# A weights' Walsh transform on one engine, and the pacing of two stages where they meet: a four-layer Mamba and sedenion network on one core

## The chip, the cores and the metric

The kernel runs on one core of a Trainium2 chip. The metric is device time in microseconds of one execution, taken as a median over runs; the median before is 10949.66 us (three runs, 10944.49 to 10950.38). The profile is of one execution with a span of 10943.5 us.

## The reference

The input x is 4 x 192 x 64 x 64, fp32. Four layers are applied to it in turn. Cut to what matters:

```python
# layer 0: tokens of 192 channels, 4096 per image, LayerNorm, then two Mambas
xs = layernorm(x.reshape(b, -1, c))
x = (xs + mamba(xs, m1) + mamba(flip(xs, -1), m2)).reshape(b, c, w, h)
# one Mamba: xz = x @ in_w.T; short causal convolution; silu; B, C, dt from x_w, dt_w; then
#   h = exp(dt * A) * h + dt * x * B ;  y = sum_n h * C       (a scan over 4096 tokens, 16 states)
# layer 1: one Mamba over tokens, then per image
x1 = x + mamba(layernorm(x))
x2 = x1 + gelu(bn(depthwise3x3(x1)))
x = x2 + mlp(layernorm(x2))            # 192 -> 768 -> 192
# layer 2: masked 3x3 depthwise convolution (4 taps), its weights made from the image's own mean
wt = (relu(bn(x.mean((2, 3)) @ w1.T)) @ w2.T + b2) * MASK
x = conv(x, wt) + bias
# layer 3: windows of 4x4, a sedenion product of the 16 window positions with 16 weights
xw = window(layernorm(x)) @ sedenion_full_weight(w_sed)
x = x + gelu(unwindow(xw)) @ proj_w + proj_b
x = x + mlp(layernorm(x))
```

The 16 x 16 sedenion product is computed as a Walsh-Hadamard convolution plus a correction for the terms whose sign differs from it. For that, the 16 weight matrices of 192 x 192 are Walsh-transformed once, each with a sign of its own; the signs of the weights are `W_SIGNS = "------------+-+-"`.

## The kernel before, in words

The program has three stages. `two_mambas` is layer 0, `mamba_block` is layer 1, and `conv_and_windows` is layers 2 and 3. Instructions are issued in an order that Python generators write out by hand; each engine (TensorE, VectorE, ScalarE, GpSimd, and the SyncE queue that issues nearly all transfers) then runs its own instructions strictly in that order, and waits for others through semaphores. So what stands behind what on one engine is decided when the program is built.

**First stage.** Units of 512 tokens go through two Mambas in turn. `Scans` issues one 128 x 512 scan at a time; work of the next units (normalisation `norm`, projections `front`, output `back`) sits in lanes of a `Behind` object and is issued between the scans. Ahead of the first scan stand the first unit's normalisation, then `at_first(work)`, which is `walsh_weights`, then the first unit's `front`.

`front` multiplies by in_w on TensorE (L456), copies the result from PSUM on ScalarE (L459), clears the halo of the convolution on GpSimd (L451) and copies it in front (L452), convolves by matmuls with diagonal weights (L474), applies silu (L486), makes dt (L500 to L509), multiplies (L510, GpSimd), and stores the rows dt and dt*x to DRAM from the SyncE queue (L515, tiles r_dt and r_dtx). `load` (L535) reads them back, spread over states, as dtE and dtxE; the first VectorE operation on them is the product L565, and the scans L578 follow.

`walsh_weights` works on four blocks: two values of i (the main 128 channels and the remaining 64, held twice) times two column halves of n = 96. For each block it loads 128 x 16 x 96 weights (L904, tile w_raw), flips the signs of the two positive ones on ScalarE (L907), then runs four butterfly stages, bits 8, 2, 1 and 4, each of one addition and one subtraction (L918), between two tiles w_walsh, and stores the result to DRAM (L922). All loads and stores are on the SyncE queue, in program order, so a block's load is issued after the store of the block before it. The blocks with i = 0 run on VectorE, those with i = 1 on GpSimd: `engine = nc.gpsimd if i else nc.vector`.

**Second stage.** Units of 512 tokens again, one Mamba. After the scan of a unit come `back` (the output projection, into a strip of image rows) and `tail`: nine depthwise matmuls for each channel half (L1044, tile ps_dw), batch norm and gelu on ScalarE (L1053, L1063), the addition on GpSimd (L1067), LayerNorm through matmuls (`NormT.run`, L294 to L341), and then `end`, the MLP (`MlpT.run`: ps_h L363, evacuation to hid L368, gelu L375, ps_o L382). Its last operation, L1079, adds the residual and accumulates the channel sums that layer 2 needs; then the tile is stored (L1090).

Between scans, `Behind.tick` issues work: it counts rounds, gives each round a TensorE budget (2.1 us here), honours the wait that a piece asks for (`Piece.wait`), and issues a deferred evacuation (`later`) when its round has come. When the scans are over, two tails and what belongs to them remain. `Behind.drain` issues these: in each round it issues everything deferred at once, forces one piece of the first lane that can go, and calls `beside` with that piece's TensorE estimate.

**Third stage.** `conv_and_windows` is a generator. When the scans are over, `mamba_block` calls `next(following)` once, which sets up its lanes, loads the first half of the first image (L1178 and L1180, tile img), makes the layer 2 weights of images 0 to 2 (`weights`), and adds `prepare(0)` to a lane. From then on these lanes share the program with the second stage's drain. `prepare(b)` handles eight groups g of two window positions: for each of three channel chunks one tap on ScalarE (helper line L1280, tile xw) and three on VectorE (L1327), then a store (L1330, kept). `first_norm` follows: mean by matmuls (helper line L1272), subtraction (L1287, L1289), square (L1290), variance by matmuls, square root (L1295), reciprocal (L1296), scaling on GpSimd (L1297, L1299), gain and sign on ScalarE (L1280, tile xn), then `both` (L1367 to L1370) and the butterfly additions `settle` (L1381, L1382). The tile img has one buffer, so the second half of an image is loaded when groups 0 to 3 have read the first.

When `drain` is through, the generator goes on: the transformed weights w_main and w_side (L1573, L1575), the untransformed ones sed (L1578) and a pack of the projections t_bw (L1161) are loaded on the SyncE queue; all eight groups of the first image are run to their end; `weights` is made for image 3 (L1203 to L1223, with the sums of the last tails); sed gets its signs on ScalarE (L1587); and `spectrum` (L1420, tile sed_ps) begins. After it come `product`, `project` and `mlp` for each group, with the next image's `prepare` in a lane beside.

The functions that the change touches, before:

Of the kernel before, what the change touches and what calls it, by code (L numbers as in the profile page):

```python
# [15 lines left out]
AF = mybir.ActivationFunctionType  # L16
ALU = mybir.AluOpType
# [105 lines left out]
def near_convolution():  # L123


    sign = sedenion_signs()
    a, b = ([1 if v == "+" else -1 for v in text] for text in (X_SIGNS, W_SIGNS))
    s, rest = [], []
    for k in range(16):
        row = [sign[i][k] * a[i] * b[i ^ k] for i in range(16)]  # L130
        s.append(1 if sum(row) >= 0 else -1)
        rest.append([i for i in range(16) if row[i] != s[k]])
    return a, b, s, rest


class Lanes:
# [24 lines left out]
    def drain(self):  # L161
        self.until(lambda: not any(self.lanes))
# [12 lines left out]
class Behind:  # L175
# [83 lines left out]
            if not any(self.try_lane(n, True, True) for n in range(len(self.lanes))):  # L259
                assert until() or self.pending, "stuck"  # L260

    def drain(self, beside=None):

        while any(self.lanes) or self.pending:
            self.now += 1
            self.issue(True)
            p = next(filter(None, (self.try_lane(n, True, True) for n in range(len(self.lanes)))), None)
            assert p or self.pending or not any(self.lanes), "stuck"
            if p and beside:
                beside(p.pe)  # L270


class NormT:
# [614 lines left out]
def walsh_weights(nc, work, w_ap, out):  # L888


    _, w_sign, _, _ = near_convolution()
    n = C // 2

    def flat(t):
        return t.rearrange("p a b -> p (a b)")[:, : 16 * n]

    def split(v, bit):
        return v.rearrange("p (h e l) -> p e h l", e=2, l=bit * n)

    for i in range(2):  # L900
        for at in range(0, C, n):
            raw = work.tile([128, 4, T], F32, name="w_raw", tag="h", bufs=3)
            v = flat(raw).rearrange("p (j c) -> p j c", c=n)
            nc.sync.dma_start(v, w_ap[:, i, :, at : at + n])  # L904
            for j in range(16):
                if w_sign[j] > 0:
                    nc.scalar.activation(v[:, j, :], v[:, j, :], AF.Copy, scale=-1.0)  # L907
            t = [flat(work.tile([128, 4, T], F32, name="w_walsh", tag="h_apart", bufs=2)) for _ in range(2)]
            src = flat(raw)
            engine = nc.gpsimd if i else nc.vector  # L910
            for m, bit in enumerate((8, 2, 1, 4)):
                a, dst = split(src, bit), t[m % 2]
                for e, op in enumerate((ALU.add, ALU.subtract)):
                    p, o = slice(0, 128), split(dst, bit)[:, e]
                    if i and bit == 4:
                        p = slice(64 * e, 64 * e + 64)
                        o = dst[p, : NP * n].rearrange("p (h l) -> p h l", h=2)
                    engine.tensor_tensor(o, a[p, 0], a[p, 1], op)  # L918
                src = dst
            rows = slice(16, 16 + NP) if i else slice(0, 16)  # L920
            k = NP if i else 16
            nc.sync.dma_start(out[:, rows, at : at + n], src[:, : k * n].rearrange("p (j c) -> p j c", c=n))  # L922


def mamba_block(tc, x, p96, p96_ap, p128, p128_ap, m_in, ex_aps, out, sums, following):
# [3 lines left out]
    nc = tc.nc  # L929
    with ExitStack() as ctx:  # L930
# [195 lines left out]
        behind.add(1, norm(units[1]))  # L1126
        Scans(nc, stream, behind).run()
        scans.close()
        lanes, passed = next(following), [0.0]

        def beside(pe):
            passed[0] += pe
            while passed[0] > 1.0:
                passed[0] -= 1.0
                lanes.tick()

        behind.drain(beside)


# [467 lines left out]
def program(ctx, tc, aps, packs, out):  # L1607
# [6 lines left out]
    def m_ins(name):  # L1614
# [8 lines left out]
        (aps["spread"], aps["gather"]),  # L1623
        x1.rearrange("b (t c) -> b t c", c=C),
        lambda work: walsh_weights(tc.nc, work, aps["sed"], walsh),
    )
    with tc.manual_schedule():
        last = conv_and_windows(tc, x2, sums, packs, aps, walsh, out)
        mamba_block(
            tc,  # L1630
            x1.rearrange("b (c t) -> b c t", t=L),
            packs["a96"],
            aps["a96"],
            packs["a128"],
            aps["a128"],
            m_ins("m"),
            (aps["spread"], aps["gather"]),
            x2,
            sums,
            last,  # L1640
        )
        for _ in last:
            pass
# [118 lines left out]
```

## Time and profile before

| what | value |
|---|---|
| median of 3 runs | 10949.66 us |
| PE, DVE, ACT, POOL busy | 84%, 83%, 60%, 65% of the span |
| 0 to 140 us: PE, DVE, ACT, POOL busy | 41.0, 24.0, 22.0, 34.9 us |
| 140 to 5410 us (first stage's scans) | DVE 5097.7 of 5270 us, granted clock 0.77 |
| 5410 to 9030 us (second stage) | PE 3261.6, DVE 2991.2 of 3620 us, clock 0.88 |
| 9030 to 9285 us (the seam to the third stage) | PE 148.1, DVE 135.1, ACT 86.8 of 255 us, clock 0.74 |
| 9285 to 10943 us (third stage) | PE 1445.4 of 1658 us, clock 0.94 |

The table's last five rows come from the profile's busy time by stretches. PE is TensorE's matmuls, DVE is VectorE, ACT is ScalarE, POOL is GpSimd, SPq is the SyncE queue. The granted clock is the share of full speed that the throttle gave TensorE. A timeline line gives start and length in us, the engine, the line of the kernel, the operation, the tile written and those read, a count where several were merged, and in brackets the idle time of the engine ahead of it with what ended it.

### The profile page before, as it was taken

How to read it: one execution, taken by the hardware profiler on the slowest of the kernel's cores; microseconds unless marked ns; L12 is line 12 of the kernel's file. 1: busy time of each engine (PE TensorE's matmuls, PEld its weight loads, DVE VectorE, ACT ScalarE, POOL GpSimd, SP SyncE). 2: the span in 40 equal slices, each digit the busy share in tenths (PEclk: the TensorE clock that was granted, in tenths of full speed). 3: DMA queues.
4: the chain of work that ended last, by engine and by line, in shares of the span. 5: the costliest groups of instructions: out<-in, count | busy, mean ns of one | idle time of the engine just before them, and what ended most of it. 6: DMA issues, size and time to landing. Idle time of an engine off the chain costs nothing. (4 is left out here: it accounts for less than half of the span.)

```text
span 10943.5 us, 97569 instructions
## 1 busy us (share of the span) xinstructions
PE 9194.5 (84%) x31352; PEld 3651.3 (33%) x31352; DVE 9081.9 (83%) x7914; ACT 6568.9 (60%) x9794; POOL 7060.3 (65%) x2704
## 2 busy tenths in 40 slices
PE   5888888888888888888678999999999986889898
PEld 1222222222222322322223333333333332445555
DVE  5999999999999999999788888888878885555552
ACT  4666666666666666666466666656656653444443
POOL 5888888888888888888666656656656661111100
PEclk7777777777777777777678989889889887999999
DMA  4666666666666666666454545545444543122110
GB/s 127 182 177 175 182 178 173 183 179 173 182 179 175 182 177 175 182 178 174 127 160 133 140 127 140 134 126 140 129 134 132 138 110 78 37 57 64 41 41 18
DMA packets 969560, 1515.13 MB, mean 138 GB/s; under 512 B 244346, under 2 KB 277150, under 8 KB 968534
## 3 DMA queue, kind: packets, MB, share of 16 engines
q1 hardware_dynamic: 968190, 1505.85, 51.3%
q8 instruction: 247, 4.05, 0.2%
q10 hardware_dynamic: 856, 3.05, 0.1%
q14 instruction: 267, 2.19, 0.1%
HBM read 1295.45 MB, written 213.12 MB: 138 GB/s over the span
## 5 line engine op out<-in xcount | busy, mean ns | idle before, releaser
L578 DVE TENSOR_TENSOR_SCAN h<-dA,m_state,h 128x512 f32<-128x512 f32 x3840 | 4669.3, 1267 | 486.3 <-ACT dA L572 424.4
L594 POOL TENSOR_TENSOR h<-h,C 128x2048 f32<-128x2048 f32 x960 | 4347.2, 4533 | 601.6 <-ACT m_state L591 496.8
L572 ACT ACTIVATE dA<-dtE,m_A 128x512 f32<-128x512 f32 x4608 | 3106.0, 687 | 1322.0 <-DVE h L578 1204.4
L565 DVE TENSOR_TENSOR h<-dtxE,B 128x2048 f32<-128x2048 f32 x960 | 2171.9, 2262 | 150.1 <-DMA dtxE<-r_dtx 137.4
L603 PE MATMUL y<-h,gather 128*32 128x512 f32 x7680 | 1286.0, 748 | 414.1 <-POOL h L594 341.7
L456 PE MATMUL ps_in<-xT,m_in_w 96*128 96x512 f32 x1536 | 943.3, 762 | 294.6 <-ACT raw L459 176.9
L1297 POOL TENSOR_TENSOR d<-d,rs 128x512 f32<-128x512 f32 x64 | 86.0, 1344 | 1604.3 <-DVE rs L1296 1583.6
L474 PE MATMUL ps_conv<-raw,m_conv 128*128 128x512 f32 x2112 | 990.7, 618 | 12.6 <-POOL raw L452 10.9
L578 DVE TENSOR_TENSOR_SCAN h_apart<-dA,m_state,h_apart 128x512 f32<-128x512 f32 x768 | 922.8, 1261 | 42.5 <-ACT dA L572 42.5
L594 POOL TENSOR_TENSOR h_apart<-h_apart,C 128x2048 f32<-128x2048 f32 x192 | 870.3, 4533 | 43.7 <-ACT m_state L591 42.3
L565 POOL TENSOR_TENSOR h_apart<-dtxE,Bs 128x2048 f32<-128x2048 f32 x192 | 892.3, 4648 | 6.0 <-ACT Bs L554 6.0
L456 PEld LDWEIGHTS ps_in<-xT,m_in_w 96*128 96x128 f32 x1536 | 352.7, 242 | 862.5 <-issue 418.0
L474 PEld LDWEIGHTS ps_conv<-raw,m_conv 128*128 128x128 f32 x2112 | 419.1, 202 | 611.0 <-issue 564.4
L593 POOL COPY m_state<-h 128x4 f32<-128x4 f32 x384 | 71.8, 187 | 850.6 <-DVE h L578 814.6
L1044 PE MATMUL ps_dw<-strip,dw 96*96 96x512 f32 x1152 | 577.0, 648 | 1.3 <-ACT x L1053 0.9
L603 PEld LDWEIGHTS y<-h,gather 128*32 128x32 f32 x7680 | 165.0, 117 | 1221.0 <-POOL h L594 540.7
L510 POOL TENSOR_TENSOR raw<-dt,xc 128x1536 f32<-128x1536 f32 x96 | 330.1, 3438 | 296.3 <-ACT dt L509 296.3
L490 PE MATMUL ps_x<-xc,m_pack 128*44 128x512 f32 x576 | 351.3, 758 | 197.7 <-ACT xc L486 194.4
L1462 PE MATMUL sed_ps<-xn,sed 64*128 64x256 f32 (+3 forms) x2944 | 486.0, 403 | 7.0 <-DVE y L1481 7.0
L572 ACT ACT_TABLE_LOAD x345 | 442.6, 1283 | 6.2
L456 PE MATMUL ps_in<-xn,m_in_w 96*128 96x512 f32 x768 | 398.5, 665 | 47.8 <-ACT z L459 31.4
L382 PE MATMUL ps_o<-hid,t 128*96 128x512 f32 x768 | 391.3, 649 | 40.0 <-ACT hid L375 19.6
(196 smaller groups left out, 12239.7 us busy)
## 6 DMA issues: line engine op xcount, KB each, us to landing
dtE<-r_dt SPq DMA_DIRECT2D x2304, 256.0 KB, 5.0
dtxE<-r_dtx SPq DMA_DIRECT2D x2304, 256.0 KB, 4.1
r_dt<-dt SPq DMA_DIRECT2D x96, 768.0 KB, 4.0
r_dtx<-raw SPq DMA_DIRECT2D x96, 768.0 KB, 5.4
x<-x SPq DMA_DIRECT2D x64, 384.0 KB, 3.9
img<-x SPq DMA_DIRECT2D x28, 512.0 KB, 8.5
xt<-in_x SPq DMA_DIRECT2D x32, 384.0 KB, 5.5
x<-o SPq DMA_DIRECT2D x32, 384.0 KB, 4.9
```

The source lines that it names most:

```text
L382: nc.tensor.matmul(ps, self.w2[:, m, bass.ts(k, CP)], h[:, m, :], start=(m == 0), stop=(m == NH - 1),)
L456: nc.tensor.matmul(ps, self.in_w[:, k, bass.ts(e, 128)], xn[:, k, :], start=(k == 0), stop=(k == 1))
L474: nc.tensor.matmul(ps, self.conv[:, d, j, :], raw[:, d, j : j + T], start=(j == 0), stop=(j == K - 1))
L490: nc.tensor.matmul(ps, self.x_w[:, d, :], xc[:, d, :], start=(d == 0), stop=(d == ND - 1))
L510: nc.gpsimd.tensor_tensor(dtx, dt, xc, ALU.mult)
L565: engine.tensor_tensor(h, u["rows", k // 2, 1], u[B, k % 2].unsqueeze(1).broadcast_to([128, 4, T]), ALU.mult)
L572: self.nc.scalar.activation(dA, u["rows", k // 2, 0][:, j, :], AF.Exp, scale=self.A[:, k, j : j + 1])
L578: self.nc.vector.tensor_tensor_scan(h[:, j, :], u.pop(("dA", k, j)), h[:, j, :], self.state[:, k, j : j + 1], ALU.mult, ALU.add,)
L594: nc.gpsimd.tensor_tensor(h, h, u["C", k % 2].unsqueeze(1).broadcast_to([128, 4, T]), ALU.mult)
L603: self.nc.tensor.matmul(u["ys"][32 * j : 32 * j + 32, :], self.ex.gather[:, i // 2, :], h[:, j, :], start=(i == 0), stop=(i == 3 and not s ...
L1044: nc.tensor.matmul(ps, dw[:, k, j, :], s[:, k, dy : dy + rows, dx : dx + HW], start=(j == 0), stop=(j == 8),)
L1462: nc.tensor.matmul(out, sed[p, int(h is not None), i ^ position(k, s), cols], xn[b, g][p, c, :], start=group(t) not in begun, stop=left[gr ...
```

## The change: all Walsh blocks on VectorE with the signs in the first stage, and a drain that uses the pace of the scans

The first part takes the transform off ScalarE and GpSimd. The sign flips disappear: where a weight of the upper half has the other sign, the addition and the subtraction of the bit 8 stage change places. That needs one pair of instructions for each run of equal signs. In the upper eight these runs are 4, 1, 1, 1, 1 long, so the stage becomes two instructions of 384 and eight of 96 elements. The four blocks all run on VectorE. It is meant to keep ScalarE and GpSimd free for the first unit's front.

The second part replaces the drain's own loop by `tick(True)`, the loop that is used between scans, with its waits, its budget and its due rounds, and gives the third stage's lanes two ticks in every round, whether or not a piece of the tails went. It is meant to mix the last tails and the third stage's first groups evenly.

```diff
-    def drain(self, beside=None):
+    def drain(self, beside=lambda: None):
         while any(self.lanes) or self.pending:
-            self.now += 1
-            self.issue(True)
-            p = next(filter(None, (self.try_lane(n, True, True) for n in range(len(self.lanes)))), None)
-            assert p or self.pending or not any(self.lanes), "stuck"
-            if p and beside:
-                beside(p.pe)
+            self.tick(True)
+            beside()
...
+    turns = [0] + [l for l in range(1, 8) if w_sign[8 + l] != w_sign[7 + l]] + [8]
+    turns = list(zip(turns, turns[1:]))
...
-            for j in range(16):
-                if w_sign[j] > 0:
-                    nc.scalar.activation(v[:, j, :], v[:, j, :], AF.Copy, scale=-1.0)
...
-            engine = nc.gpsimd if i else nc.vector
             for m, bit in enumerate((8, 2, 1, 4)):
                 a, dst = split(src, bit), t[m % 2]
+                if bit == 8:
+                    for first, last in turns:
+                        at_l, ops = slice(n * first, n * last), (ALU.add, ALU.subtract)
+                        for e, op in enumerate(ops[::-1] if w_sign[8 + first] > 0 else ops):
+                            nc.vector.tensor_tensor(
+                                split(dst, bit)[:, e, 0, at_l], a[:, 0, 0, at_l], a[:, 1, 0, at_l], op
+                            )
+                    src = dst
+                    continue
...
-                    engine.tensor_tensor(o, a[p, 0], a[p, 1], op)
+                    nc.vector.tensor_tensor(o, a[p, 0], a[p, 1], op)
...
-        lanes, passed = next(following), [0.0]
-
-        def beside(pe):
-            passed[0] += pe
-            while passed[0] > 1.0:
-                passed[0] -= 1.0
-                lanes.tick()
+        lanes = next(following)
+
+        def beside():
+            lanes.tick()
+            lanes.tick()
```

More of the change, by code (lines that the diff above doesn't have):

```diff
@@ L892, in walsh_weights @@
     n = C // 2
+    assert max(w_sign[:8]) < 0
+    turns = [0] + [l for l in range(1, 8) if w_sign[8 + l] != w_sign[7 + l]] + [8]
+    turns = list(zip(turns, turns[1:]))
     def flat(t):
```

## The prediction

> **What bounds the kernel now.** I read the page's 40 slices first: no engine bounds the whole span. Up to slice 19 DVE stands at 9, then PE and DVE share, and from slice 34 PE stands at 8 to 9. The two stretches that the change touches are the seams before and between these regimes, where the average shares say nothing, so I read the timeline there.
>
> First seam, 0 to 140 us. The timeline of all engines (start, length, engine, line and operation, then the idle time before it and its releaser):
>
> ```profile
> 25.49 5.96 PE L456 MATMUL ps_in<-xT,m_in_w 96*128 96x512 f32 x8
> 28.53 5.55 DVE L918 TENSOR_TENSOR w_walsh<-w_walsh 128x768 f32<-128x768 f32 x6
> 34.52 1.68 SPq L904 DMA_DIRECT2D w_raw<-in_sed  x1
> 42.05 0.46 ACT L907 ACTIVATE w_raw<-w_raw 128x96 f32<-128x96 f32 x2 [15.41 <-DMA w_raw<-in_sed]
> ...
> 62.06 10.92 POOL L918 TENSOR_TENSOR w_walsh<-w_walsh 128x768 f32<-128x768 f32 x6
> ...
> 79.73 0.46 ACT L907 ACTIVATE w_raw<-w_raw 128x96 f32<-128x96 f32 x2 [21.39 <-DMA w_raw<-in_sed]
> 80.09 1.05 ACT L459 COPY raw<-ps_in 128x512 f32<-128x512 f32 x2
> ...
> 94.90 0.37 SPq L922 DMA_DIRECT2D walsh<-w_walsh  x1
> 94.93 0.11 POOL L451 MEMSET m_halo<- 128x9 f32 x1
> ...
> 95.35 12.04 PE L474 MATMUL ps_conv<-raw,m_conv 128*128 128x512 f32 x24 [10.86 <-POOL raw L452]
> ```
>
> To see: the first Mamba unit's projection (ps_in) is done on PE at 31.5, but its copy out of PSUM stands on ACT behind the fourth block's sign flips (79.73) and goes at 80.09; the halo memset stands on POOL behind the fourth block's additions and goes at 94.93. So the unit's convolution starts at 95.35. From there, in the same view, r_dt is issued at 122.63 and the first product L565 runs at 138.59, from which on DVE is loaded.
>
> Second seam, from the end of the second stage's scans (9026) to the first spectrum matmul (9285.28):
>
> ```profile
> 9145.42 14.73 SPq L1180 DMA_DIRECT2D img<-x  x8
> ...
> 9200.94 0.69 DVE L1287 TENSOR_TENSOR d<-xw,mean 128x512 f32<-128x512 f32 x1
> ...
> 9217.79 0.69 DVE L1287 TENSOR_TENSOR d<-xw,mean 128x512 f32<-128x512 f32 x1
> ...
> 9250.52 0.69 DVE L1287 TENSOR_TENSOR d<-xw,mean 128x512 f32<-128x512 f32 x1
> ...
> 9279.19 0.45 PE L1212 MATMUL ps_se<-pooled,t_b 96*48 96x1 f32 x4 [23.06 <-DVE pooled L1209]
> 9280.08 5.28 PE L1220 MATMUL ps_wt<-se,w 48*128 48x1 f32 x24 [0.44 <-ACT se L1215]
> 9285.28 2.08 PE L1420 MATMUL sed_ps<-xh,w_main 128*128 128x256 f32 x4
> ```
>
> To see: each of the third stage's eight groups g has one subtraction L1287. They start at 9078.2, 9097.0, 9141.3, 9173.0, 9200.9, 9217.8, 9235.4, 9250.5. While the tails are being issued (to 9200) a group takes 19 to 44 us, afterwards 15 to 18. The tails' last output leaves at 9200.34 and the groups then run on alone for 65 us. The busy time by stretches gives, from 9043.5 to 9285.3 (241.8 us), DVE 133 and PE 135 us: both half idle, so this is a chain of waits and not a full engine.
>
> **What the Trainium skill says.** VectorE: DVE Perf Modes, the section on the TRN2 errata, prices an fp32 tensor_tensor at (N+151)/0.96 ns: 957 ns at N=768, and L918 on DVE has 956; at 96 and 384 it gives 257 and 557 ns, shapes that this trace lacks. GPSIMD Engine Reference, 3.1, has the same operation 1.96 times slower on POOL; here 1800 against 956 ns is 1.88. DMA: Bandwidth & Descriptors, in the anatomy of one DMA, says that a wait is held by the issuing sequencer before dispatch: in the trace each w_raw load stands behind the store of the block before (34.11 then 34.52). TensorE: Matmul & The Clock Gate, Part 1, has an idle PE fall to half rate; the granted clock here is 0.50 from 35 to 50 us and at times in the second seam.
>
> **The change, part by part.**
>
> *Walsh transform.* Removed: 8 flips L907 on ACT and 16 additions on POOL (2 x 14.5 us). Added on DVE: two more blocks, and in each block the stage of bit 8 is 10 instructions (2 of 384, 8 of 96 elements) instead of 2 of 768. By the formula 2 x 0.557 + 8 x 0.257 = 3.17 us; six L918 of 955 ns take 5.55, so neighbours overlap by 30 ns, which leaves 2.9 us. Bounds: 2.1 us, if small ones overlap as the 128x2 aggregates do (0.18 long, 0.10 apart), to 3.2. A block is 2.9 + 5.55 = 8.45 us.
> The chain is now: DVE free after the normalisation's last aggregate at 20.2 (the first w_raw landed 8.8 us after 6.43, at 15.2); block 0 to 28.65; store, then load 0.4 later, 29.1; landing 7.5 us (34.52 to 42.05), 36.6; block 1 to 45.1; load 45.6, landed 53.1; block 2 to 61.6; load 62.1, landed 6.2 later (73.49 to 79.73) at 68.3; block 3 to 76.8; last store 76.9; SP free 77.3.
> Behind the waiting SP stand r_dt and r_dtx of the first unit. Its front now runs beside this: copies at 27 to 35, convolution from about 35; before it took 27.3 us from convolution to r_dt (95.35 to 122.63) and 3.6 more to r_dtx: 62 and 66, before 77.3 even with some more half-clock matmuls. So r_dt goes at 77.3 instead of 122.63: 45.3 us earlier. What follows (r_dt landing, spread loads, product) keeps its order and durations. DVE has nothing else queued before that product. Take 45, bounds 38 (slow small additions and landings) to 49.
>
> *Drain.* Nothing is removed; the 94 matmul instructions of the last two tails and the eight groups are put in another order. The old loop gives the lanes a tick for each 1.0 us of the tails' PE estimate, and pieces without PE work give none; the new one gives two ticks each round whether or not a tail moves, and a round admits about 2.1 us of PE work. The instruction order shows the effect: on PE the first two groups' means and the first variance now stand with the first tail's norm, and the last group's variance stands before the last four ps_o matmuls; on DVE both last sums L1079 stand between group 7's reciprocal and the settling additions. Tails and groups end together.
> I carried the times through the new order by hand with durations of the seam: tap 0.68, subtraction 1.55 in all, sq 0.84, rs 0.69, reciprocal 3.35, POOL 3.3, xn 1.6, swaps 0.8, tail norm halves 1.22, gelu 2.76, table load 1.28, second image load 9 us to its first part and 15 to its second (9145.42 to 9154.56 and 9160.68). Subtractions come at 9062, 9080, 9101, 9127 (image load, issued 9105 instead of 9145), 9152, 9170, 9188, 9207. Check: seven gaps of 17 us, as without tails, are 119; 10 of image wait, 8 of tail work on DVE and 8 of gelu and table loads on ACT make 145, and 9062 + 145 = 9207. From the last subtraction to the first settling addition were 15.1 us (9250.5 to 9265.6): 9222 against 9265.6, 44 us earlier.
> Given back: the third stage's weights (7 MB) are queued behind the tails' last store, now at 9222 instead of 9200. Before, issue to the landing of the last was 17.5 us with 3 us of wait ahead; sed then lands near 9222 + 3 + 14 = 9239, when its flips on ACT are due (9222 + 14 = 9236), and the next batch's image, behind them in the queue, lands its first part at about 9249, where the first spectrum copy on ACT was due at 9222 + 25 = 9247. That costs about 3 us. Half-clock matmuls that I entered at full rate: 3 more. Take 38, bounds 12 to 50, for a hand-carried chain of 250 us.
>
> Sum: 45 + 38 = 83; 10949.7 - 83 = 10866.7, say 10867.
>
> **Rivals.**
> A. The drain gives nothing: ACT and PE stall on the tails in program order (a gelu of 2.76, six hid copies), each group takes 22 to 26 us, and late weights hold the spectrum. For it: groups took 19 to 44 us beside tails before. Against: 65 us of tail-free groups at the end are what it can fill. Seven gaps of 24.5 put the last subtraction at 9234; 6 us more given back, and 10 lost in the next batch's groups: no gain, 10905.
> B. The drain gives all: gaps of 17.6 and no further image wait, last subtraction near 9195, 55 us: 10849.
> C. Slower: the fine additions on DVE take as long as POOL did, the front still waits (gain 10), and the drain's late weights and image stall the spectrum's copies: tails end at 9300, spectrum at 9325, a loss of 40. Net 30 slower: 10980. Against it: L459 and L451 stand behind nothing of the transform any more.
>
> **How the numbers follow.** Forecast 0.70, A 0.15, B 0.10, C 0.05. I leave out C and half of the outer tails: 10842 to 10908. Faster by over 0.2% means under 10927.8: all but C and some of A's tail, 0.92; same 0.03; slower 0.05.
>
> **What would show it.** In the changed profile: r_dt issued near 77 (over 85: my DVE block or the landings are wrong; if what ends its wait is ACT or POOL, the front is the bound); first product near 93; everything through the two scan stages shifted by 45; the last group's subtraction 145 us after the first; first spectrum matmul some 83 us earlier than 9285.3, with less than 5 us of waiting on ACT for weights or image after it. If the spectrum's start gains but the end doesn't, the third stage has another bound, and I am wrong on the carry-through.

## The result, and the profile after

| | before | after |
|---|---|---|
| median (four runs each; before: the three named above and one more) | 10947.08 us | 10869.17 us (10868.44 to 10876.5) |
| ratio to before, 95% interval | | 0.9931 [0.9913, 0.9948] |
| span of the profiled run | 10943.5 us | 10866.7 us |
| PE, DVE, ACT, POOL busy | 9194.5, 9081.9, 6568.9, 7060.3 us | 9179.8, 9098.4, 6566.6, 7032.3 us |

The change takes 77.9 us off the median and 76.8 us off the profiled span, while the busy time of the engines hardly moves: 16.5 us more on DVE and 27.9 us less on POOL, about what the two moved blocks take there. What went is waiting, in the two seams. The kernel before was timed again beside each group of experiments, with medians from 10943.76 to 10947.08 us, so a difference of 3 us between kernels that were not timed side by side means little. In the changed kernel's line numbers the transform is L913 (stage of bit 8) and L923, its store L927, r_dt L511, the product L561; in the second seam the group's mean is L1275, its subtraction L1290, settle L1384 and L1385, the tails' last sum L1084, the spectrum L1423 and its first copy out of PSUM L1426.

First seam. In the kernel before, r_dt and the first product stand here:

```profile
122.63 0.37 SPq L515 DMA_DIRECT2D r_dt<-dt  x1
...
138.59 2.29 DVE L565 TENSOR_TENSOR h<-dtxE,B 128x2048 f32<-128x2048 f32 x1 [88.65 <-DMA dtxE<-r_dtx]
```

The changed kernel, timeline of all engines:

```profile
20.00 2.34 DVE L913 TENSOR_TENSOR w_walsh<-w_raw 128x384 f32<-128x384 f32 x10
22.38 5.55 DVE L923 TENSOR_TENSOR w_walsh<-w_walsh 128x768 f32<-128x768 f32 x6
...
28.37 1.69 SPq L904 DMA_DIRECT2D w_raw<-in_sed  x1
...
34.47 10.47 PE L470 MATMUL ps_conv<-raw,m_conv 128*128 128x512 f32 x24
...
36.01 2.38 DVE L913 TENSOR_TENSOR w_walsh<-w_raw 128x384 f32<-128x384 f32 x10 [8.07 <-DMA w_raw<-in_sed]
...
59.55 1.48 ACT L505 ACTIVATE dt<-dt 128x1536 f32<-128x1536 f32 x1
...
74.72 0.37 SPq L927 DMA_DIRECT2D walsh<-w_walsh  x1
75.18 0.53 SPq L511 DMA_DIRECT2D r_dt<-dt  x1
...
91.35 2.29 DVE L561 TENSOR_TENSOR h<-dtxE,B 128x2048 f32<-128x2048 f32 x1 [16.66 <-DMA dtxE<-r_dtx]
```

To see: the convolution starts at 34.47 instead of 95.35, since neither ScalarE nor GpSimd has transform work ahead of it. dt is done at 61.03 (59.55 + 1.48), but its store r_dt goes only at 75.18, directly behind the transform's last store at 74.72, in the SyncE queue. So the chain of the transform (load, ten short additions, six long ones, store, load) still sets the start of the scans, now 47.2 us earlier.

Second seam. In the kernel before, its first load, the tails' last sum and the spectrum's first copy out of PSUM:

```profile
9027.41 0.36 SPq L1161 DMA_DIRECT2D t_bv<-in_bv  x1
...
9199.52 0.74 DVE L1079 SCALAR_TENSOR_TENSOR x<-ps_o,t,x 96x512 f32<-96x512 f32 x1
...
9290.64 0.77 ACT L1423 ACTIVATE xh<-sed_ps 64x256 f32<-64x256 f32 x2 [9.06 <-PE sed_ps L1420]
```

The changed kernel, the same view:

```profile
8977.95 0.36 SPq L1164 DMA_DIRECT2D t_bv<-in_bv  x1
...
9135.90 8.42 PE L359 MATMUL ps_h<-xn,t 96*128 96x512 f32 x12 [8.11 <-ACT xn L337]
...
9145.93 0.69 DVE L1290 TENSOR_TENSOR d<-xw,mean 128x512 f32<-128x512 f32 x1 [4.57 <-PE mean L1275]
...
9155.74 2.76 ACT L371 ACTIVATE hid<-hid 128x3072 f32<-128x3072 f32 x1
...
9158.56 7.31 PE L378 MATMUL ps_o<-hid,t 128*96 128x512 f32 x12 [4.86 <-ACT hid L371]
...
9167.48 0.69 DVE L1290 TENSOR_TENSOR d<-xw,mean 128x512 f32<-128x512 f32 x1 [6.14 <-PE mean L1275]
...
9181.02 0.74 DVE L1084 SCALAR_TENSOR_TENSOR x<-ps_o,t,x 96x512 f32<-96x512 f32 x1
...
9185.90 1.13 SPq L1581 DMA_DIRECT2D sed<-in_sed  x2
...
9201.33 2.08 PE L1423 MATMUL sed_ps<-xh,w_main 128*128 128x256 f32 x4
9202.87 0.94 ACT L1590 ACTIVATE sed<-sed 128x384 f32<-128x384 f32 x2 [6.80 <-DMA sed<-in_sed]
...
9212.28 0.84 ACT L1283 ACTIVATE xw<-img,t_bv,wt 128x256 f32<-128x256 f32 x1 [8.47 <-DMA img<-x]
9213.14 0.77 ACT L1426 ACTIVATE xh<-sed_ps 64x256 f32<-64x256 f32 x2
```

To see: the last sum of the tails (9181.02) now comes behind the last group's subtraction, and the spectrum follows 20 us later; no group runs on alone. Before, four groups came after the last sum. The last two subtractions wait for a mean that stands behind ps_h and ps_o on PE. And the first copy of the spectrum, which before came 5.4 us after the first spectrum matmul (9285.28, 9290.64), comes 11.8 us after it: ScalarE stands 6.8 us for sed and 8.5 us for the next image. Both are queued behind the tails' last store (L1095, issued at 9181.92).

The seam is read below from its first load (t_bv on SPq: 9027.41 before, 8977.95 after) to the first copy. From the first copy on hardly anything has changed; the busy time by stretches (from, to, length, then busy time and instructions of each engine, granted clock, DMA share, GB/s) has, before and after:

```profile
9290.64:10943.00 1652.36, 1439.71 (x7920) 882.42 (x7920) 831.74 (x1189) 665.96 (x928) 171.02 (x175) 0.94 0.18 43
```

```profile
9213.14:10866.00 1652.86, 1439.54 (x7904) 881.65 (x7904) 833.43 (x1192) 666.21 (x928) 171.08 (x175) 0.94 0.18 44
```

So the span's difference of 76.8 us splits as follows: 47.2 up to the first product (138.59 to 91.35), 2.2 from there to the seam (8888.8 to 8886.6), 28.0 in the seam (263.2 to 235.2), and 0.7 lost after it.

### The profile page after: what moved, and what is told of

It is laid out like the page before. It is cut to its first block, busy times and chain, and to the rows that moved or that the text cites. A ratio compares the mean times of both kernels' runs of the same rounds, so it can differ in the third digit from the quotient of the medians.

```text
span 10866.7 us, 97590 instructions
## 1 busy us (share of the span) xinstructions
PE 9179.8 (84%) x31352; PEld 3644.1 (34%) x31352; DVE 9098.4 (84%) x7962; ACT 6566.6 (60%) x9784; POOL 7032.3 (65%) x2688
## 5 line engine op out<-in xcount | busy, mean ns | idle before, releaser
L561 DVE TENSOR_TENSOR h<-dtxE,B 128x2048 f32<-128x2048 f32 x960 | 2170.6, 2261 | 78.6 <-DMA dtxE<-r_dtx 65.9
L561 POOL TENSOR_TENSOR h_apart<-dtxE,Bs 128x2048 f32<-128x2048 f32 x192 | 889.6, 4633 | 6.0 <-ACT Bs L550 6.0
```

What stands on the lines that cost most here:

```text
L561: engine.tensor_tensor(h, u["rows", k // 2, 1], u[B, k % 2].unsqueeze(1).broadcast_to([128, 4, T]), ALU.mult)
```

## The experiments

Each diff is against the changed kernel and cut to its main lines. "Seam" is the second seam, and its times are from the t_bv load.

**The two parts alone.** The first keeps the new transform with the old drain, the second the old transform with the new drain.

```diff
# e1_walsh_only
-            self.tick(True)
-            beside()
+            self.now += 1
+            self.issue(True)
+            p = next(filter(None, (self.try_lane(n, True, True) for n in range(len(self.lanes)))), None)
+            if p and beside:
+                beside(p.pe)
...
# e2_drain_only
-                    nc.vector.tensor_tensor(o, a[p, 0], a[p, 1], op)
+            for j in range(16):
+                if w_sign[j] > 0:
+                    nc.scalar.activation(v[:, j, :], v[:, j, :], AF.Copy, scale=-1.0)
+            engine = nc.gpsimd if i else nc.vector
+                    engine.tensor_tensor(o, a[p, 0], a[p, 1], op)
```

> The Walsh part alone, with the old drain. Theory (the two seams add): r_dt is issued near 75 us instead of 122.6, everything behind it moves by 47 to 50 us, the seam to the third stage keeps its old length of 258 us from its start to the first spectrum matmul: 49 us faster than before, about 10898. Rival (the parts interact, because the shift changes how the seam falls): the seam's length changes by over 5 us, and the time lies under 10890 or over 10906.

> The new drain alone, with the old Walsh transform. Theory (the seams add): r_dt stays at 122.6 us, the seam shortens by about 34 us at the first spectrum matmul, of which about 7 are given back before the first copy of a spectrum, since the copy waits for sed and for the next image: 27 us faster than before, about 10920. Rival (nothing is given back): 34 us, about 10913.

Measured, beside 10944.63 for the kernel before: e1 10895.79 us, ratio 0.9957 [0.9940, 0.9973], a gain of 48.8; e2 10916.37 us, ratio 0.9975 [0.9965, 0.9985], a gain of 28.3. The sum, 77.1, is what the whole change brings: the parts don't interact. In e1 the first product is at 91.33 and the seam is 258.0 us to the first spectrum matmul, as before (257.9). In e2 the product is at 137.86 and the seam is 223.8 us, as with the whole change (223.4).

**What in the transform's move counts.** The first of these leaves all blocks on VectorE but gives the flips back to ScalarE; the second folds the signs in but leaves the i = 1 blocks on GpSimd.

```diff
# e3_flips_on_act
+            for j in range(16):
+                if w_sign[j] > 0:
+                    nc.scalar.activation(v[:, j, :], v[:, j, :], AF.Copy, scale=-1.0)
-                if bit == 8:
...
# e4_half_on_pool
+            engine = nc.gpsimd if i else nc.vector
-                            nc.vector.tensor_tensor(
+                            engine.tensor_tensor(
...
-                    nc.vector.tensor_tensor(o, a[p, 0], a[p, 1], op)
+                    engine.tensor_tensor(o, a[p, 0], a[p, 1], op)
```

> As the changed kernel, but the signs are still flipped on ScalarE ahead of each block (all additions stay on VectorE). Theory (what counts is what stands ahead of the front on ScalarE): the front's copies of ps_in stand behind the fourth block's flips at about 73 us, the convolution starts near 77 and r_dt goes near 105: 30 us slower than the changed kernel, about 10899. Rival (what counts is only the speed of the additions): r_dt goes when the SyncE queue is free, near 81 us, about 10875.

> As the changed kernel with its signs within the additions, but the two blocks of i = 1 run on GpSimd as before. Theory (what counts is what stands ahead of the front on GpSimd): the halo memset stands behind the fourth block on GpSimd, near 90 us, so the convolution starts there and r_dt goes near 117: 42 us slower than the changed kernel, about 10911. Rival (the flips on ScalarE were the hold, GpSimd only made the transform longer): r_dt goes when the SyncE queue is free, near 90 us, 15 us slower, about 10884.

Measured: e3 10901.85 us, ratio 0.9962 [0.9947, 0.9977]; e4 10912.83 us, ratio 0.9971 [0.9960, 0.9983]. The timeline of e3:

```profile
72.64 0.46 ACT L903 ACTIVATE w_raw<-w_raw 128x96 f32<-128x96 f32 x2 [14.09 <-DMA w_raw<-in_sed]
73.00 1.05 ACT L455 COPY raw<-ps_in 128x512 f32<-128x512 f32 x2
...
80.66 0.37 SPq L918 DMA_DIRECT2D walsh<-w_walsh  x1
...
104.21 0.37 SPq L511 DMA_DIRECT2D r_dt<-dt  x1
```

The two flips of the fourth block take 0.46 us, but the unit's copy out of PSUM stands behind them, and they wait 14.09 us for the load. r_dt then comes 23.5 us behind the transform's last store: the front is the later one here, and it is late because two short instructions wait. The timeline of e4:

```profile
74.70 4.69 POOL L914 TENSOR_TENSOR w_walsh<-w_raw 128x384 f32<-128x384 f32 x10 [6.53 <-DMA w_raw<-in_sed]
79.46 10.92 POOL L924 TENSOR_TENSOR w_walsh<-w_walsh 128x768 f32<-128x768 f32 x6
...
90.44 0.11 POOL L447 MEMSET m_halo<- 128x9 f32 x1
...
90.86 13.29 PE L470 MATMUL ps_conv<-raw,m_conv 128*128 128x512 f32 x24 [56.30 <-POOL raw L448]
...
120.30 0.37 SPq L511 DMA_DIRECT2D r_dt<-dt  x1
```

Here a memset of 0.11 us stands behind the fourth block on GpSimd, and PE has been idle for 56.30 us when the copy behind that memset (L448) lets the convolution start. So each half of the move alone leaves most of the wait: with e4 the first product is 2.4 us earlier than before, with e3 18.8, with both 47.2. Their gains don't add, since both stand ahead of the same front and the later one decides.

**Is it now the queue?** The first three loads are issued at once, the fourth ahead of the first block's store, when the first of the three buffers of w_raw is free.

```diff
# e6_prefetch
+    for _ in range(3):
+        fetch()
...
-            nc.sync.dma_start(v, w_ap[:, i, :, at : at + n])
+            raw = raws[2 * i + at // n]
...
+            if len(raws) < 4:
+                fetch()
```

> As the changed kernel, but the first three w_raw blocks are loaded at once and the fourth after the first block's store. Theory (the SyncE queue, blocked by each store in turn, sets r_dt): VectorE runs the four blocks without the 22 us of waiting for loads, from 20 to 52 us, the queue is free near 53, and r_dt goes when the front has it, near 61: 14 us earlier than 75, the time near 10855. Rival (the load's traffic or the front holds r_dt): the front gets slower and r_dt stays over 70, the time 10865 or more.

Measured: 10855.26 us (10854.5 to 10857.95), ratio 0.9919 [0.9905, 0.9932], 13.9 less than the changed kernel (13.7 between the profiled spans). The timeline of e6:

```profile
51.86 5.64 DVE L932 TENSOR_TENSOR w_walsh<-w_walsh 128x768 f32<-128x768 f32 x6 [0.59 <-DMA walsh<-w_walsh]
...
59.26 1.48 ACT L505 ACTIVATE dt<-dt 128x1536 f32<-128x1536 f32 x1
60.77 0.36 SPq L511 DMA_DIRECT2D r_dt<-dt  x1
...
76.49 2.29 DVE L561 TENSOR_TENSOR h<-dtxE,B 128x2048 f32<-128x2048 f32 x1 [18.98 <-DMA dtxE<-r_dtx]
```

The transform is over at 57.5, not at 52 as expected: VectorE waits 4.9 us in all for stores of w_walsh, which has two buffers. r_dt goes 0.03 us after dt is done: now the front is the bound. In the changed kernel dt was just as early (61.0), and 14 us of queue lay between.

**What was given back behind the seam.** sed and the pack t_bw are loaded behind the first group's spectrum, and the flips of sed come after all eight.

```diff
# e5_late_sed
-        for i in range(2):
-            nc.sync.dma_start(sed[:, i], aps["sed"][:, i])
-        w |= pack("bw", nc.sync, const)
...
+                if b == g == 0:
+                    for i in range(2):
+                        nc.sync.dma_start(sed[:, i], aps["sed"][:, i])
+                    w |= pack("bw", nc.sync, const)
```

> As the changed kernel, but sed and the projections' pack are loaded after the first group's spectrum is issued, so behind the next image's first half, and sed's flips stand after all eight spectra. Theory (what the drain gives back is the wait of ScalarE for sed and for the image behind 7 MB): the first copy of a spectrum starts 5 to 6 us after the first spectrum matmul, as before the change, instead of 11.8, and the time falls by about 6 us, to 10863. Rival (the spectrum's copies have slack before the products): no change, 10869, because the next image's taps or the products set the pace.

Measured: 10864.84 us (10860.67 to 10865.22), ratio 0.9926 [0.9912, 0.9939]. The timeline of e5:

```profile
9200.68 0.84 ACT L1283 ACTIVATE xw<-img,t_bv,wt 128x256 f32<-128x256 f32 x1 [4.77 <-DMA img<-x]
9201.17 2.08 PE L1423 MATMUL sed_ps<-xh,w_main 128*128 128x256 f32 x4
...
9206.21 2.78 SPq L1594 DMA_DIRECT2D sed<-in_sed  x2
...
9206.55 0.77 ACT L1426 ACTIVATE xh<-sed_ps 64x256 f32<-64x256 f32 x2 [5.02 <-PE sed_ps L1423]
```

The first copy is again 5.4 us behind the first matmul, 6.6 us earlier than in the changed kernel, and its wait is for PE, no longer for a transfer. So some 6 us were given back to late loads, and the seam can have them again. The total shows 4.3 of them, hardly more than the scatter between sessions. Between the two profiled runs the rest is found behind the first copy: the third stage takes 1656.7 us from there instead of 1653.5, with the same matmuls busy for 1443.7 us instead of 1439.5, at a granted clock of 0.93 instead of 0.94. It need not come from the edit, since e10 below has the same late loads and 1652.7 us there.

**Both together.** e10_both has the edits of e5 and e6.

> The late loads of sed and the early loads of w_raw together in the changed kernel. Theory: the two gains add, about 20 us, 10849. Rival (either gain is swallowed by what follows): only one of the two shows, 10855 to 10863.

Measured: 10850.61 us (10847.51 to 10855.45), ratio 0.9914 [0.9901, 0.9928]: 18.6 less than the changed kernel, where e5 and e6 alone give 4.3 and 13.9. Beside e6, timed in the same session, the late loads bring 4.7 us. It is the fastest version here, ahead of both kernels; the seam is 229.1 us to the first copy.

**Rounds or pace.** The new drain changes two things: the rounds in which the tails' pieces go, and how often the third stage's lanes get a tick. Four kernels take them apart.

```diff
# e7_forced_two: the old forcing round, two ticks in each
-            self.tick(True)
+            self.now += 1
+            self.issue(True)
+            p = next(filter(None, (self.try_lane(n, True, True) for n in range(len(self.lanes)))), None)
...
# e8_tick_by_pe: the new rounds, one tick for each 1.0 us of the tails' PE estimate
...
+        def beside(pe):
+            passed[0] += pe
+            while passed[0] > 1.0:
+                passed[0] -= 1.0
+                lanes.tick()
...
# e9_ticks_1: the new rounds, one tick in each
-            lanes.tick()
...
# e9_ticks_3: the new rounds, three ticks in each
+            lanes.tick()
```

> The changed kernel with the old forcing loop in the drain (all deferred work at once, one piece a round, no waits and no budget), but with two ticks of the lanes in every round, as in the new one. Theory (the gain is that groups and tails end together, so the number of ticks while the tails last is what counts, not the waits): groups and tails are mixed about as in the change and the time stays within 8 us of 10869. Rival (the waits and due rounds of the scans' pace keep the engines from blocking each other): the seam is longer by 10 us or more, over 10879.

> The changed drain's rounds (tick, which also admits by due time), but the groups paced as before: one tick for each 1.0 us of the tails' PE estimate. Both last sums then stand on DVE between the third and the fourth group's subtraction, and four groups come after the last tail. Theory (what counts is how many groups still stand after the last tail): as the kernel before in this seam, first spectrum matmul 250 to 260 us after the seam's start, total 10890 to 10900. Rival (the new rounds of the tails themselves bring the gain, not the pace): within 5 us of the changed kernel's 10869.

> One tick for the groups in each round instead of two. The last sums stand between the third and fourth group, four groups are left alone after them. Theory: 250 to 260 us from the seam's start to the first spectrum matmul, total 10890 to 10900, as with ticks by PE. Rival (a gain of the rounds): 10864 to 10874.

> Three ticks in each round: all eight groups stand ahead of the last tail's sums, which come after the last group's subtraction. Theory: the groups end earlier, but the tail then runs alone at its own latency and the third stage's weights are queued behind its last store, so the weights come late: the spectrum's first copy waits for sed by over 10 us; total 10872 to 10900, slower than the changed kernel. Rival (the tails are short, groups first is best): 10855 to 10868.

Measured, with the seam from the traces:

| kernel | us | ratio to before, 95% | last sum after seam start | groups whose subtraction comes after it | to the first spectrum matmul | to its first copy |
|---|---|---|---|---|---|---|
| before | 10947.08 | | 172.1 | 4 | 257.9 | 263.2 |
| e8_tick_by_pe | 10894.32 | 0.9954 [0.9939, 0.9969] | 167.2 | 4 | 254.1 | 259.4 |
| e9_ticks_1 | 10886.43 | 0.9947 [0.9932, 0.9962] | 152.7 | 4 | 252.1 | 257.0 |
| e7_forced_two | 10886.78 | 0.9948 [0.9934, 0.9961] | 198.9 | 2 | 249.5 | 254.0 |
| after | 10869.17 | 0.9931 [0.9913, 0.9948] | 203.1 | 0 | 223.4 | 235.2 |
| e9_ticks_3 | 10911.43 | 0.9969 [0.9959, 0.9980] | 243.7 | 0 | 259.4 | 275.6 |

All rows but the first have the new transform, so they compare with e1's 10895.79. My expectation of e7 fell and its rival held: the pace alone brings 9 of the 27 us. e8 shows that the new rounds alone bring next to nothing (1.5 us of the total, 4 in the seam); e9_ticks_1 came out 4 us under its range, with the seam inside it, and e9_ticks_3 11 us above. Of these orders, only the one in which tails and groups end together has the short seam. With one tick the tails are through at 152.7 with four groups still to come, and the spectrum starts 99 us later; with three ticks the groups are through and a whole MLP runs alone. The timeline of e9_ticks_3:

```profile
9161.65 0.69 DVE L1291 TENSOR_TENSOR d<-xw,mean 128x512 f32<-128x512 f32 x1 [4.52 <-PE mean L1276]
...
9189.43 1.21 DVE L330 TENSOR_TENSOR xn<-xn,rb 96x1024 f32<-96x1024 f32 x1
...
9191.55 13.97 PE L359 MATMUL ps_h<-xn,t 96*128 96x512 f32 x24 [12.45 <-ACT xn L337]
...
9218.33 0.75 DVE L1084 SCALAR_TENSOR_TENSOR x<-ps_o,t,x 96x512 f32<-96x512 f32 x1 [27.69 <-PE ps_o L378]
```

All groups' subtractions are issued by 9161.65. The last tail's normalisation (L330) stands on DVE behind the settling additions and goes at 9189.43; then only the tail runs. Its last store comes late, so the loads queued behind it do too: ScalarE stands 16.9 us for sed, the last 6 of them after the first spectrum matmul.

**The gaps before the last two groups.** The ticks go ahead of the tails' round instead of behind it, so that the last groups' mean stands behind fewer matmuls of ps_h and ps_o.

```diff
# e11_beside_first
-            self.tick(True)
-            beside()
+            beside()
+            self.tick(True)
```

> The changed kernel, with the third stage's two ticks ahead of the tails' round instead of behind it. On PE the last two groups' mean then stands behind 4 matmul instructions of ps_h and of ps_o instead of 6, and the earlier groups' one piece earlier too. Theory (the two gaps of 22 us before the last two subtractions, where DVE waits 4.57 and 6.14 us for PE's mean behind ps_h and ps_o, are what my working missed): these two waits shrink by 1 to 3 us each, the seam from its start to the first spectrum matmul is 217 to 222 us instead of 223.4, total 10862 to 10868. Rival (the tails' own chain of MLP, gelu and PE sets these gaps, whatever stands first): seam 222 to 226, total within 3 us of 10869; if the tails' last sums come later by more than the groups gain, slower.

Measured: 10884.05 us (10882.24 to 10885.34), ratio 0.9943 [0.9930, 0.9957]: 15 us slower than the changed kernel, so neither my theory nor the rival's figure held, though the rival had named this way to be slower. The timeline of e11:

```profile
9162.82 1.09 ACT L1283 ACTIVATE xn<-d,norm 128x256 f32<-128x256 f32 x2 [0.87 <-POOL d L1302]
9163.94 0.82 ACT L1370 COPY swapped<-xn 64x256 f32<-64x256 f32 x2
...
9164.78 0.69 ACT L364 ACTIVATE hid<-ps_h,t 128x512 f32<-128x512 f32 x1
9165.49 1.28 ACT L371 ACT_TABLE_LOAD   x1
9166.78 2.76 ACT L371 ACTIVATE hid<-hid 128x3072 f32<-128x3072 f32 x1
9169.59 6.70 PE L378 MATMUL ps_o<-hid,t 128*96 128x512 f32 x8 [8.46 <-ACT hid L371]
9176.13 1.66 PE L1275 MATMUL mean<-xw,ones 128*128 128x256 f32 x8
...
9177.91 0.69 DVE L1290 TENSOR_TENSOR d<-xw,mean 128x512 f32<-128x512 f32 x1 [12.63 <-PE mean L1275]
```

The gelu comes at 9166.78 instead of 9155.74, ps_o waits for it on PE (8.46 us), and the last group's mean waits behind ps_o. Of these 11 us, 4.0 are there when the tail's MLP starts (its scaling L337 at 9139.00 instead of 9135.03), and the last 3.6 come where a group's gain and sign (xn), waiting for GpSimd, stand on ScalarE ahead of the tail's last hid copy (9164.78); what makes the rest was not taken apart. So the wait that I wanted to shrink grew from 6.14 to 12.63 us, although only 8 ps_o matmuls stand ahead of the mean instead of 12: what counts there is when the gelu comes. The seam is 234.3 us to the first matmul, and the weights, queued at 9200 instead of 9186, add 4.2 us more wait up to the first copy than in the changed kernel. e7's trace has the same order, gelu behind xn, with 4 ps_o matmuls ahead of the mean and a wait of 8.86 us for it.

## Why the prediction was right, point by point

The direction, the two places and the chains that I gave for them held. That the time is so close (10867 forecast, 10869.17 measured) is partly luck. The gain was 77.9 us and not 83: the drain brought 10 less than forecast, and 2.2 more from the Walsh transform and 2.2 of scatter ahead of the second seam made up for some of it. Another 2.6 us of the closeness come from the median before, 10949.66 when the forecast was made and 10947.08 with a fourth run. Of the signs that I named, r_dt near 77 (75.18) and the first product near 93 (91.35) came; the last group's subtraction came 154 us after the first instead of 145, and ScalarE's waits, forecast under 5 us, were 6.80 and 8.47. The first spectrum matmul came 84.0 us earlier, as said, but as 47.2 + 2.2 + 34.5.

*Walsh transform: 45 forecast, 47.2 measured at the first product.* The mechanism is shown by e3, e4 and e6: the front had stood behind flips and GpSimd additions, and the transform's own chain is what is left. The step that was off is the stage of bit 8, taken as 2.9 us: it takes 2.34 to 2.38, so a block is 7.9 us and not 8.45, and four of them make r_dt 75.18 instead of 77.3. The formula that the Trainium skill gives (VectorE: DVE Perf Modes, the section on the TRN2 errata) makes an estimate of 257 and 557 ns at 96 and 384 elements, and single instructions agree, with 251 and 551 ns here. Their sum does not price the stage: neighbours overlap, by more than I had read from the long ones, though within the bounds that I gave (2.1 to 3.2 us). The front before the queue was also as I had it: dt was ready at 61.0, against my 62. The further 2.2 us that the trace shows up to the second seam are no gain of the change: the stretch from product to seam runs from 8885.0 to 8890.6 us over the fourteen traces of this study, both kernels included.

*Drain: 38 forecast, 28 measured.* With the seam's start laid over that of before, the eight subtractions come at 9062.9, 9081.3, 9102.4, 9127.6, 9155.3, 9173.1, 9195.4 and 9216.9; I had 9062, 9080, 9101, 9127, 9152, 9170, 9188 and 9207. Up to the fourth, with the image's wait in it, this is right within 2 us. Of the 10 us at the end, 3 come before the fifth, and 7 from the last two gaps, which are 22 us instead of 18 and 19: the mean of a group stands on PE behind a tail's ps_h and, for the last one, behind ps_o that waits for the gelu. I had counted these tails as work on DVE (8 us) and on ACT (8 us), and not as a place in PE's order. That the last gap grows when the gelu comes later is shown by e11; whether a finer mix of ps_h and the means would win the 7 us back wasn't tried. From the last subtraction to settle is 14.2 us (15.1 forecast) and from there to the first spectrum matmul 19.6, as before. The matmul comes 34.5 us earlier in the seam instead of 44. The 3 us that I took off for matmuls at half clock can't be told apart from these gaps.

*Given back: 3 forecast, 6.4 measured.* The mechanism, weights and image queued behind a later store, is shown by e5. The size was off in the landings, counted here from the first settling addition. sed was to be issued 3 us after it and to land 14 us later; its two loads were issued at 4.2 and 5.0 and landed 16.2 us later. The image's first part was put at 27 us and was there at 30.6: one of its issues (9188.30, L1183) stood on the SyncE queue for 16.87 us behind the weights, where in e5, with sed and t_bw out of the way, the same issue took 8.29.

*The rivals.* A (the drain gives nothing) and B (all of it) are both out by e2, which has 28.3 us. C is out by e1: the fine additions don't cost what they did on GpSimd. The Trainium skill (GPSIMD Engine Reference, 3.1) has GpSimd 1.96 times slower at an fp32 addition of 2048 elements. Shorter ones lie closer together here: in e4 1800 against 955 ns at 768 elements, or 1.88, and 385 against 251 at 96, or 1.53. The bit 8 stage as a whole took 4.69 us there against 2.36, or 1.99.

*The carry-through.* The third stage after the first copy has the same length within 0.7 us, so what the spectrum's copies gained the end gained. Over all traces this stretch lies between 1652.3 and 1660.0 us, so a gain of a few us in the seam need not show in one run.

## What to carry to other kernels

A job of two instructions and half a microsecond can cost as much as it waits for, when work on the critical chain stands behind it: look on each engine for cheap work that waits for a transfer ahead of such work, and remove all these places at once, since one that is left keeps most of the wait. When two streams are merged by hand, count what is left of either one after the last piece of the other, and then look on every engine, PE included, at which instruction of one stream stands behind a waiting instruction of the other. Moving the end of a stage forward also moves its weights' loads against their first use, so check what is queued behind the last store before counting the gain.

## What had not been expected of the hardware

The ten short additions of a stage (sum of durations 8 x 0.251 + 2 x 0.551 = 3.11 us) took 2.34 to 2.38 us, so each overlaps the next by some 83 ns; six of 768 elements (6 x 0.955 = 5.73 us) took 5.55 to 5.64, 18 to 36 ns each. On GpSimd the same ten (8 x 0.385 + 2 x 0.991 = 5.06 us) took 4.69, some 41 ns each. What sets the difference was not looked into.
